# A hub stage with its startup, its loads and its row saves in another order

## The chip, the cores and the metric

The kernel runs on one core of a Trainium2 chip (trn2). The metric is device time in microseconds of one launch. The runs give a median and a range, and one more execution is taken by the hardware profiler; the profile and its trace come from that one. Engines are called as the profile calls them: PE (matrix multiply), PEld (its weight load), DVE (vector), ACT (scalar), POOL (GpSimd) and SP (which here only issues DMAs). "SPq" and "ACTq" are the DMA-issuing instructions on SP and ACT.

## The reference

The input is x (8 batches, 2048 nodes, 64 channels) and a 2048 x 2048 adjacency matrix whose entries are dense among the low-numbered nodes and sparse elsewhere. One layer of two-level graph attention is added to x, and the sum is layer-normalised:

```
mask = graph + eye(N) > 0
h = einsum('bnc,hdc->bhnd', x, Wh)              # 4 heads
out_h = softmax(where(mask, h h^T, -1e16)) h + bh
z = leaky_relu(concat of heads);  h2 = z Wo^T
out2 = softmax(where(mask, h2 h2^T, -1e16)) h2 + bo
y = layernorm(leaky_relu(out2)) * gamma + beta
result = layernorm(x + y)
```

## The kernel before

The kernel uses the sparsity. The first 56 nodes ("hub" nodes, `HUB`) attend to every node and are computed densely. The other 1992 nodes are grouped into 166 sets of 12, and for each set only up to 128 listed neighbours are fetched with an indirect DMA. There are three stages, one after the other: the hub stage (it also builds the neighbour lists), the first layer for the sets (83 pairs of sets), and the second layer. The order on each engine is the order in which the Python code issues instructions; there is no scheduler, and each engine runs its own queue in order.

**The hub stage** begins with loads. `load_x(i)` (line 449) allocates a tile of 128 nodes from a ring of ten row tiles, sets its border columns on DVE (line 451) and issues two DMAs on ACT's queue (line 453), each of 128 KB in contiguous stretches of 64 floats. `save_x(i)` (line 457) writes that tile from SP to `table1` in DRAM, from which the second stage gathers; until that write has landed, the tile's place in the ring can't be reused. Before the loop four x tiles are loaded, then `hubraw` (the adjacency rows of the hubs, line 465), the weights `wnat` and `wos` (lines 467 and 468).

`load_adj` (line 669) loads one piece of the adjacency matrix of the sets (480 KB) through SP into a ring of three `raw` buffers, which the two `hubraw` tiles share; POOL turns it into a 0/1 bf16 tile `a` (line 680) and, on each second piece, sets the diagonal (line 687). The `a` tiles come from a ring of five, which `hubm` and `hubs` share. `more(n)` issues the next n pieces. Twelve pieces make a round of 60 sets; there are 34 pieces in three rounds.

Ahead of the loop, in this order: `more(2)`; `hub_mask` (the hubs' 0/1 mask `hubm` on DVE, line 541, 16 turning matmuls into `pm`, line 545, and the two halves of `maskh`, line 548); `hub_mask_sets` (a strided copy `hubs` on ACT, line 559, 17 turning matmuls into `pms`, line 562, and `maskt`, line 566, which only the last stage reads); `weights` (lines 497 to 506: `gram`, `whT`, `woT`); `turn_x(0)` (transposes of x tile 0 into `xT`, lines 512 and 583); `hub_columns` (line 575, `yh`).

The loop has 16 iterations of two halves t. A half is `hub_scores` (matmuls `sh`, line 590; the mask subtracted on DVE, line 594, called the lift here; exp on ACT, line 597) and, one half later, `hub_values` (matmuls `oh`, line 608, into the accumulators `hubo`). Around them:

```
        if i + 4 < NB:
            load_x(i + 4)
        more(2 if i < 7 else 1)
        save_x(i)
        ...
            if t == 1 and i in (3, 6):
                make_keys(0, (i - 3) // 3, two)
                if i == 6:
                    picks = pick(0)
            if t == 1 and i in (9, 15):
                make_keys(1, (i - 9) // 6, two)
            some(3)
```

`make_keys` (line 712) packs six pieces into half of a round's keys with matmuls `pk` (line 721) and two DVE instructions (line 708). `pick(0)` (line 727) is a list of 39 DVE jobs that extract each set's neighbours: 32 with MAX8 (line 737), most of them with MATCH_REPLACE8 (line 739), one merge, one that writes `index` (line 766) and five that write `mask` (line 777). `some(3)` runs three jobs per half. After the loop the rest of the jobs run, six gathers are issued from `table1` on POOL (line 792), `own_rows` copies columns of `xT` on POOL (line 800), and `hub_end` closes the accumulators (lines 616 and 617). PSUM in this stage has two double-bank tiles with tag "s" (all short uses) and two with tag "o" (`hubo`).

Of the kernel before, what the change touches and what calls it, by code (L numbers as in the profile page):

```python
# [36 lines left out]
OP = mybir.AluOpType  # L37
# [7 lines left out]
HUB = 56  # L45
SET = 12
# [313 lines left out]
def fast_kernel(ctx: ExitStack, tc: tile.TileContext, x, adj, Wh, bh, Wo, bo, gamma, beta, out, flag):  # L360


    nc = tc.nc
    B, N, C = x.shape
    H, D, _ = Wh.shape
    P = 128
# [7 lines left out]
    NS = (N - HUB) // SET  # L374
# [20 lines left out]
    def two(name, tag="s", **kw):  # L395

        return psum.tile([P, 2, 512], F32, tag=tag, name=name, **kw)
# [27 lines left out]
    table1 = dram.tile([N, ROW], F32, name="table1")  # L425
# [11 lines left out]
    maskh = const.tile([P, NB, HUB * H], U8, name="maskh")  # L437
# [8 lines left out]

    xrow = {}

    def load_x(i):
        t = xrow[i] = rows_tile(f"x{i}")  # L450
        nc.vector.memset(t[:, :, 0:PW:PW - 1], 1.0)
        for p in range(2):
            nc.scalar.dma_start(out=t[:, :, 1 + p * D:1 + (p + 1) * D],
                                in_=x[p::2, i * P:(i + 1) * P, :].rearrange("q n c -> n q c"))

    def save_x(i):
        nc.sync.dma_start(out=table1[i * P:(i + 1) * P, :], in_=xrow[i].rearrange("n q c -> n (q c)"))
# [28 lines left out]
                                compare_op=OP.not_equal, fill=float(1 << k))  # L486
    number = early.tile([P, 2, HALFN], U16, name="number")
    nc.gpsimd.iota(number, [[1, 2], [2, SEG // 2], [SEG, HALFN // (SEG // 2)]], base=0, channel_multiplier=0)
    load_x(2)
    load_x(3)  # L490

    def weights():
        pw = two("pw")
        for h in range(H):
            for r in range(2):
                w = wnat[half(r), h, :]
                nc.tensor.matmul(pw[half(r), r, h * D:(h + 1) * D], w, w, start=True, stop=True)
                nc.tensor.matmul(pw[half(r), r, (H + h) * D:(H + h + 1) * D], w, ident[half(r), half(r)],
                                 start=True, stop=True)
        for r in range(2):  # L500
            nc.vector.tensor_copy(gram[half(r), :, half(r)], pw[half(r), r, :H * D].rearrange("c (h e) -> c h e", h=H))
            nc.scalar.copy(whT[half(r), :], pw[half(r), r, H * D:])
        po = two("po")
        for hp in range(HP):
            nc.tensor.matmul(po[:, 0, hp * D:(hp + 1) * D], wos[:, hp * P:(hp + 1) * P], ident[:D, :D], start=True, stop=True)
        nc.vector.tensor_copy(woT.rearrange("p q d -> p (q d)"), po[:, 0, :HP * D])
# [28 lines left out]
    hubm = early.tile([HUB, N], BF16, tag="a", name="hubm", bufs=5)  # L535
    HW = HUB * H
    HV = HW // 4

    def hub_mask():
        for k in range(2):  # L540
            nc.vector.tensor_scalar(hubm[:, k * NCH:(k + 1) * NCH], hubraw[k], 1.0, 0.0, OP.min, OP.max)
        nc.vector.tensor_tensor(hubm[:, :HUB], hubm[:, :HUB], identb[:HUB, :HUB], OP.max)
        pm = two("pm")
        for m in range(NB):
            nc.tensor.matmul(pm[:, m // 8, (m % 8) * HUB:(m % 8 + 1) * HUB], hubm[:, m * P:(m + 1) * P],
                             identb[:HUB, :HUB], start=True, stop=True)
        for k in range(2):
            nc.vector.tensor_scalar(
                maskh[:, k * 8:(k + 1) * 8, :].rearrange("p m (n h) -> p (m n) h", h=H),
                pm[:, k, :8 * HUB].unsqueeze(2).to_broadcast([P, 8 * HUB, H]), 0.0, 255.0, OP.is_equal, OP.mult)  # L550

    def hub_sets(b):

# [2 lines left out]
    def hub_mask_sets():  # L556
        pm = two("pms")
        cols = early.tile([HUB, NS * SET], BF16, tag="a", name="hubs", bufs=5)
        nc.scalar.copy(cols.rearrange("n (s k) -> n s k", k=SET), hubm[:, HUB:].rearrange("n (k s) -> n s k", s=NS))
        for b in range(NHB):  # L560
            s0, ns = hub_sets(b)
            nc.tensor.matmul(pm[:ns * SET, b // 9, b % 9 * HUB:(b % 9 + 1) * HUB], cols[:, s0 * SET:(s0 + ns) * SET], identb[:HUB, :HUB],
                             start=True, stop=True)
        for b0, n in ((0, 9), (9, NHB - 10), (NHB - 1, 1)):
            np_ = hub_sets(b0)[1] * SET
            nc.vector.tensor_scalar(maskt[:np_, b0:b0 + n, :].rearrange("p b n -> p (b n)"),
                                    pm[:np_, b0 // 9, b0 % 9 * HUB:(b0 % 9 + n) * HUB], 0.0, 255.0, OP.is_equal, OP.mult)
# [3 lines left out]
    def hub_columns():  # L571
        py = two("pyh")
        for t in range(2):
            for h in range(H):
                nc.tensor.matmul(py[:, t, h * 2 * HUB:(h + 1) * 2 * HUB], gram[:, h, :],
                                 xT[:, 2 * t:2 * t + 2, :HUB], start=True, stop=True)
            nc.vector.tensor_copy(yh[:, t, :].rearrange("p (n h) -> p n h", h=H),
                                  py[:, t, :H * 2 * HUB].rearrange("p (h n) -> p n h", h=H))

    def turn_x(i):  # L580
        tp = two(f"px{i}")
        turn(tp[:, 0, :], xrow[i])
        nc.scalar.copy(xT[:, :, i * P:(i + 1) * P], tp[:, 0, :].rearrange("c (q n) -> c q n", q=Q))
# [12 lines left out]
                                maskh[:, i, :].unsqueeze(1).unsqueeze(1).to_broadcast([P, 2, 2, HW]), OP.subtract)  # L596
        nc.scalar.activation(e, e, AF.Exp, bias=shifts[:, 0:1], scale=1.0)  # L597

    hubo = [two(f"oh{t}", "o") for t in range(2)]

    def hub_values(i, t):

# [109 lines left out]
    def make_keys(r, t3, new):  # L712

        n = in_round[r]
        groups = [(t, min(S10, n - S10 * t)) for t in range(3 * t3, min(3 * t3 + 3, (n + S10 - 1) // S10))]
        pk = new(f"pk{r}_{t3}")
        for h in range(2):
            c = (2 * t3 + h) * 32
            for b in range(2):
                for i, (t, ns) in enumerate(groups):  # L720
                    nc.tensor.matmul(pk[c:c + 32, b, :], powers_of(ns, t % 3), ahead[r, t][:ns * SET, h, b * 512:(b + 1) * 512],
                                     start=(i == 0), stop=(i == len(groups) - 1), tile_position=(0, c))
        for h in range(2):
            part = slice((2 * t3 + h) * 32, (2 * t3 + h + 1) * 32)
            keep_keys(keys[r % 2][part, :], pk[part], part, h)
# [64 lines left out]
    def gather(table, s, layer, new):  # L790
        t = rows[layer, s] = new(f"g{layer}_{s}")
        nc.gpsimd.indirect_dma_start(out=t.rearrange("n q c -> n (q c)"), out_offset=None, in_=table,  # L792
                                     in_offset=bass.IndirectOffsetOnAxis(ap=index[:, s:s + 1], axis=0))
# [139 lines left out]
    def more(n):  # L933

        for _ in range(n):
            if pieces:
                load_adj(*pieces.pop(0))

    more(2)
    hub_mask()  # L940
    hub_mask_sets()
    weights()
    turn_x(0)
    hub_columns()
    picks = []

    def some(n):
        for _ in range(n):
            if picks:
                picks.pop(0)()  # L950

    def turns():
        return bool(picks) and getattr(picks[0], "turns", False)

    for e in es:
        nc.vector.memset(e[:, 4 * HW:], 1.0)
    pend = None
    for i in range(NB):
        if i + 4 < NB:
            load_x(i + 4)  # L960
        more(2 if i < 7 else 1)
        save_x(i)
        if i == 2:
            nc.gpsimd.memset(rall[:, NG:, :], 1.0)
            nc.gpsimd.memset(rall2, 1.0)
            nc.gpsimd.memset(over, 0.0)
            for k in range(SET):
                nc.gpsimd.memset(bits[:, k:k + 1], N << k)
            nc.gpsimd.memset(shifts[:, 2:3], EPS)
            nc.gpsimd.memset(ones, 1.0)  # L970
            for t in rowts + xbs:
                nc.gpsimd.memset(t, 1.0)
            if last:
                make_powers6()
        for t in range(2):
            hub_scores(i, t)
            if t == 0 and i + 1 < NB:
                turn_x(i + 1)
            if pend:
                hub_values(*pend)  # L980
            pend = i, t
            if t == 1 and i in (3, 6):
                make_keys(0, (i - 3) // 3, two)
                if i == 6:
                    picks = pick(0)
            if t == 1 and i in (9, 15):
                make_keys(1, (i - 9) // 6, two)
            some(3)
    hub_values(*pend)
    while picks:  # L990
        picks.pop(0)()
    LOOK = 5
    for g in range(LOOK - 2):
        for j in range(2):
            gather(table1, 2 * g + j, 1, rows_tile)
    own_rows(0)
    own_rows(1)
    for t in range(2):
# [14 lines left out]
    picks = pick(1)  # L1013
# [3 lines left out]
    for i in range(-4, NG + 3):  # L1017
# [10 lines left out]
        if 0 <= i + 2 < NG:  # L1028
            t = held["T", 1, i + 2] = work.tile([P, 2, 512], F32, tag="xTg", name=f"xTg{i + 2}", bufs=3)
# [16 lines left out]
        if i >= 0:  # L1046
# [9 lines left out]
            if not picks and not todo3 and done < NS:  # L1056
                picks = pick(2)
# [376 lines left out]
```

## Time and profile before

| what | us |
|---|---|
| median of 3 runs (range) | 1047.05 (1044.12 to 1052.09) |
| the profiled execution, its own time | 880.76 |
| its span, first to last instruction | 878.9 |
| busy: PE, DVE, ACT, POOL | 753.0, 610.1, 514.4, 469.2 |
| hub stage in the trace | 0 to 144.4 |
| first matmul of `weights` (line 497) | 20.55 |
| first lift (line 594) | 32.78 |
| first pick (line 737) | 77.19 |
| first lift after the last pick job | 125.78 |
| last lift of the hub stage | 137.22 |

The profiled execution is 166 us shorter than the median of the runs. In the trace a line of the timeline gives start, duration, engine, source line, operation, the tile written and read, the count, and in brackets the idle time of that engine before it with what released it. A line of the busy table gives, for a stretch of time, the busy time of each engine with its count of instructions, then the clock granted to PE, the share of time in which the 16 DMA engines were busy, and the rate.

### The profile page before, as it was taken

How to read it: one execution, taken by the hardware profiler on the slowest of the kernel's cores; microseconds unless marked ns; L12 is line 12 of the kernel's file. 1: busy time of each engine (PE TensorE's matmuls, PEld its weight loads, DVE VectorE, ACT ScalarE, POOL GpSimd, SP SyncE). 2: the span in 40 equal slices, each digit the busy share in tenths (PEclk: the TensorE clock that was granted, in tenths of full speed). 3: DMA queues.
4: the chain of work that ended last, by engine and by line, in shares of the span. 5: the costliest groups of instructions: out<-in, count | busy, mean ns of one | idle time of the engine just before them, and what ended most of it. 6: DMA issues, size and time to landing. Idle time of an engine off the chain costs nothing.

```text
span 878.9 us, 42066 instructions
## 1 busy us (share of the span) xinstructions
PE 753.0 (86%) x18437; PEld 661.2 (75%) x18437; DVE 610.1 (69%) x1369; ACT 514.4 (59%) x961; POOL 469.2 (53%) x612
## 2 busy tenths in 40 slices
PE   1896777889999999999999999992999999998730
PEld 1664456778788999988999999971899999988720
DVE  3356983568888788877555555553258999998994
ACT  2342333556556667666766667651678888886821
POOL 5654141457444555655666666503777777777300
PEclk9998998999999999999999999995999999999965
DMA  8787451355434445655566665514888888888611
GB/s 167 238 218 213 129 146 48 83 142 160 109 100 118 112 125 159 162 169 153 160 168 173 160 166 162 134 28 114 246 266 253 275 275 267 266 252 242 172 46 35
DMA packets 81794, 145.22 MB, mean 165 GB/s; under 512 B 30146, under 2 KB 46466, under 8 KB 81602
## 3 DMA queue, kind: packets, MB, share of 16 engines
q0 software_dynamic: 26720, 88.55, 36.4%
q1 hardware_dynamic: 37842, 49.65, 18.7%
q10 hardware_dynamic: 17040, 4.25, 2.6%
q8 instruction: 147, 2.41, 1.1%
q14 instruction: 45, 0.37, 0.1%
HBM read 123.91 MB, written 18.48 MB: 162 GB/s over the span
## 4 chain that ended last, share of the span: by engine, by line
PE 63%; DVE 15%; DMA 7%; ACT 5%; issue 4%; SPq 3%; POOL 2%; DVEq 0%; ACTq 0%; POOLq 0%
PE t L512 11%; PE s L821 10%; PE o L846 10%; PE cat L806 6%; PE o L863 4%; PE cat L531 4%; PE cat L880 3%; PE s L1133 3%; PE o L1165 3%; PE cat L890 2%; DMA raw<-in_adj_dram 2%; SPq L1248 2%; PE sh L1277 2%; PE e L1144 2%; DMA g<-table,index 1%
## 5 line engine op out<-in xcount | busy, mean ns | idle before, releaser
L792 POOL DMA_INDIRECT g<-table,index x332 | 334.9, 1009 | 236.1 <-PE o L846 140.2
L512 PE MATMUL t<-ident,g 128*128 128x128 f32 x1328 | 182.3, 276 | 15.6 <-DMA g<-table,index 12.7
L512 PEld LDWEIGHTS t<-ident,g 128*128 128x128 f32 x1328 | 154.8, 142 | 20.0 <-issue 14.0
L826 DVE TENSOR_TENSOR e<-s,mask 128x768 f32<-128x768 f32 x83 | 79.4, 956 | 87.4 <-PE s L821 85.4
L518 ACT ACTIVATE z<-cat,bhp 128x192 f32<-128x192 f32 x166 | 60.8, 418 | 85.0 <-PE cat L531 85.0
L846 PE MATMUL o<-g,e 128*64 128x65 f32 x2656 | 97.5, 227 | 0.0
L821 PEld LDWEIGHTS s<-y,xTg 64*64 64x64 f32 x5312 | 85.2, 134 | 13.9 <-issue 13.7
L821 PE MATMUL s<-y,xTg 64*64 64x48 f32 x5312 | 95.5, 220 | 0.0
L846 PEld LDWEIGHTS o<-g,e 128*64 128x64 f32 x2656 | 85.8, 140 | 9.8
L1320 ACT COPY xTg<-t 128x1024 f32<-128x1024 f32 x83 | 80.3, 1017 | 18.1 <-PE t L512 17.3
L1030 ACT COPY xTg<-t 128x1024 f32<-128x1024 f32 x83 | 84.0, 1012 | 2.0 <-PE t L512 2.0
L833 ACT ACTIVATE e<-e,shifts 128x768 f32<-128x768 f32 x83 | 79.2, 955 | 2.1 <-DVE e L826 1.7
L812 ACT COPY y<-cat 128x384 f32<-128x384 f32 (+1 forms) x80 | 40.7, 508 | 64.0 <-PE o L863 40.1
L597 ACT ACTIVATE e<-e,shifts 128x896 f32<-128x896 f32 x32 | 33.4, 1042 | 73.0 <-DVE e L594 52.1
L680 POOL TENSOR_SCALAR a<-raw 120x1024 bf16<-120x1024 int32 (+1 forms) x34 | 38.2, 1125 | 65.1 <-DMA raw<-in_adj_dram 38.4
L806 PE MATMUL cat<-xo,gram 128*128 128x192 f32 (+1 forms) x320 | 65.6, 328 | 0.0
L853 DVE RECIPROCAL rall<-o 64x8 f32<-64x8 f32 x166 | 34.0, 205 | 42.0 <-PE o L846 40.7
L854 DVE TENSOR_TENSOR osb<-o,rall 128x512 f32<-128x512 f32 x83 | 57.4, 692 | 2.9
L1165 PE MATMUL o<-g,es 128*32 128x65 f32 x2656 | 49.1, 226 | 5.9 <-DVE y_s L1188 4.5
L806 PEld LDWEIGHTS cat<-xo,gram 128*128 128x128 f32 x320 | 53.7, 203 | 0.3 <-issue 0.2
L1165 PEld LDWEIGHTS o<-g,es 128*32 128x32 f32 x2656 | 46.1, 113 | 7.0 <-issue 4.9
L1133 PE MATMUL s<-xTg,bd 128*32 128x128 f32 x1328 | 45.4, 277 | 6.2 <-ACT bd L1124 3.5
(177 smaller groups left out, 1369.3 us busy)
## 6 DMA issues: line engine op xcount, KB each, us to landing
raw<-in_adj_dram SPq DMA_DIRECT2D x32, 480.0 KB
table<-xb SPq DMA_DIRECT2D x22, 256.0 KB
xr_s<-table SPq DMA_DIRECT2D x21, 256.0 KB
g<-table,index POOLq DMA_INDIRECT x332
table<-x SPq DMA_DIRECT2D x16, 260.0 KB
x<-in_x_dram ACTq DMA_DIRECT2D x32, 128.0 KB
table<-rowt SPq DMA_DIRECT2D x166, 24.4 KB
xb<-in_x_dram SPq DMA_DIRECT2D x164, 24.0 KB
```

Source lines behind the costliest of these rows:

```text
L512: nc.tensor.transpose(tp[:, q * P:(q + 1) * P], rows[:, q, 1:1 + P], ident)
L518: nc.scalar.activation(z[:, hp], cat[:, :, hp * n:(hp + 1) * n], AF.Identity, bias=bhp[:, hp:hp + 1], scale=1.0)
L792: nc.gpsimd.indirect_dma_start(out=t.rearrange("n q c -> n (q c)"), out_offset=None, in_=table, in_offset=bass.IndirectOffsetOnAxis(ap=ind ...
L806: nc.tensor.matmul(cat[:, k, 2 * GM:2 * GM + n], gram[:, g % 2 * 2 + k, :], held["x", g // 2][:, :n], start=True, stop=True)
L821: nc.tensor.matmul(sp[half(r), p, (q * 2 + j) * M:(q * 2 + j + 1) * M], xt[half(p), j, q, half(r)], y[half(p), (j * Q + q) * M:(j * Q + q ...
L826: nc.vector.tensor_tensor(e[:, :16 * M].rearrange("p (a q n) -> p a q n", a=2, q=Q), sp[:, :, :8 * M].rearrange("p a (q n) -> p a q n", q= ...
L833: nc.scalar.activation(e[:, :16 * M], e[:, :16 * M], AF.Exp, bias=shifts[:, 0:1], scale=1.0)
L846: nc.tensor.matmul(op[half(p), j, o0:o0 + K1], e[:, c0:c0 + 64], rw[j][:, q, sums(p)], start=True, stop=True)
L1030: nc.scalar.copy(t, held.pop(("tp", i + 2)))
L1133: nc.tensor.matmul(sp[q * 32:(q + 1) * 32, k, :], bd[u % 3][:, k, q, :], xt[:, s % 2, q, :], start=True, stop=True, tile_position=(0, q * 32))
L1165: nc.tensor.matmul(op[t * 32:(t + 1) * 32, f, k * W2 + p:k * W2 + p + K1], e[:, 2 * q + p, k, :], rw[:, q, sums(p)], start=(a == 0 and k = ...
L1320: nc.scalar.copy(t, tp)
```

## The change

- `load_x` takes an optional queue. Tiles 2 and 3 are issued on SP, each after one of the first two adjacency pieces; the other tiles stay on ACT.
- `hub_mask_sets` moves from before the loop to the end of iteration 1, and its strided copy goes from ACT to DVE.
- `pm` takes a PSUM tile of tag "o"; the two DVE instructions that make `maskh` are split: one goes after `weights`, one after `hub_columns`. The accumulators `hubo` are allocated after that.
- Adjacency pieces: 2 in iterations 0, 2, 4 and 7 to 12, 1 in iterations 1, 3, 5 and 6, none from 13. So 12 have been issued by iteration 6 and 24 by the end of the loop (before: 16 and 25).
- `save_x` is delayed: tiles 0 to 3 in iterations 5 to 8, then two tiles in each of iterations 9 to 14.
- `make_keys` runs in iterations 3, 8, 11 and 15, so that `pick(0)` starts in iteration 8; `some` takes four jobs per half.
- The first six gathers are issued in iteration 14.

```diff
-    def load_x(i):
+    def load_x(i, queue=None):
...
-            nc.scalar.dma_start(out=t[:, :, 1 + p * D:1 + (p + 1) * D],
+            (queue or nc.scalar).dma_start(out=t[:, :, 1 + p * D:1 + (p + 1) * D],
...
-    load_x(2)
-    load_x(3)
...
+    maskp = []
...
-        pm = two("pm")
+        pm = two("pm", "o")
+        maskp.append(pm)
...
-        for k in range(2):
-            nc.vector.tensor_scalar(
-                maskh[:, k * 8:(k + 1) * 8, :].rearrange("p m (n h) -> p (m n) h", h=H),
-                pm[:, k, :8 * HUB].unsqueeze(2).to_broadcast([P, 8 * HUB, H]), 0.0, 255.0, OP.is_equal, OP.mult)
+
+    def hub_mask_half(k):
+        nc.vector.tensor_scalar(
+            maskh[:, k * 8:(k + 1) * 8, :].rearrange("p m (n h) -> p (m n) h", h=H),
+            maskp[0][:, k, :8 * HUB].unsqueeze(2).to_broadcast([P, 8 * HUB, H]), 0.0, 255.0, OP.is_equal, OP.mult)
...
-        nc.scalar.copy(cols.rearrange("n (s k) -> n s k", k=SET), hubm[:, HUB:].rearrange("n (k s) -> n s k", s=NS))
+        nc.vector.tensor_copy(cols.rearrange("n (s k) -> n s k", k=SET), hubm[:, HUB:].rearrange("n (k s) -> n s k", s=NS))
...
-    hubo = [two(f"oh{t}", "o") for t in range(2)]
+    hubo = []
...
-    more(2)
+    more(1)
+    load_x(2, nc.sync)
+    more(1)
+    load_x(3, nc.sync)
     hub_mask()
-    hub_mask_sets()
     weights()
+    hub_mask_half(0)
     turn_x(0)
     hub_columns()
+    hub_mask_half(1)
+    hubo.extend(two(f"oh{t}", "o") for t in range(2))
     picks = []
+    save_at = {i: range(i - 5, i - 4) if i < 9 else range(2 * i - 14, 2 * i - 12) for i in range(5, 15)}
...
-        more(2 if i < 7 else 1)
-        save_x(i)
+        more(2 if i in (0, 2, 4) or 7 <= i < 13 else 1 if i < 7 else 0)
+        for k in save_at.get(i, ()):
+            save_x(k)
...
-            if t == 1 and i in (3, 6):
-                make_keys(0, (i - 3) // 3, two)
-                if i == 6:
+            if t == 1 and i in (3, 8):
+                make_keys(0, i // 8, two)
+                if i == 8:
                     picks = pick(0)
-            if t == 1 and i in (9, 15):
-                make_keys(1, (i - 9) // 6, two)
-            some(3)
+            if t == 1 and i in (11, 15):
+                make_keys(1, i // 4 - 2, two)
+            if t == 1 and i == 1:
+                hub_mask_sets()
+            some(4)
+        if i == 14:
+            while picks:
+                picks.pop(0)()
+            for g in range(LOOK - 2):
+                for j in range(2):
+                    gather(table1, 2 * g + j, 1, rows_tile)
     hub_values(*pend)
-    while picks:
-        picks.pop(0)()
-    LOOK = 5
-    for g in range(LOOK - 2):
-        for j in range(2):
-            gather(table1, 2 * g + j, 1, rows_tile)
```

More of the change, by code (lines that the diff above doesn't have):

```diff
@@ L953, in turns @@
         return bool(picks) and getattr(picks[0], "turns", False)
+    LOOK = 5
     for e in es:
```

## The prediction, made before the changed kernel ran

> **What bounds the kernel now.** I read first the busy table over the stages, because the change touches only the hub stage (0 to 144.4 us); then DVE's, ACT's and PE's timelines inside it; then the queue's own waits.
>
> ```profile
> 0.00:31.00 31.00, 10.96 (x93) 9.61 (x93) 8.75 (x17) 6.18 (x5) 16.92 (x39) 1.00 0.83 188
> 31.00:75.00 44.00, 38.15 (x701) 25.96 (x704) 18.95 (x27) 17.80 (x21) 21.85 (x61) 0.96 0.83 232
> 75.00:126.00 51.00, 36.20 (x665) 25.74 (x657) 47.35 (x125) 15.34 (x18) 15.08 (x20) 0.93 0.48 142
> 126.00:144.40 18.40, 13.84 (x292) 9.82 (x288) 10.53 (x14) 7.20 (x8) 5.10 (x7) 0.97 0.31 89
> ```
>
> Columns: stretch, length, then PE, PEld, DVE, ACT, POOL busy. The stage has four parts with different limits. To 31 us no compute engine is the limit: the startup waits for loads (DMA 0.83 busy). From 31 to 75, PE is busy 38 of 44: this part is PE's, with a few stalls. From 75 to 126, DVE is busy 47 of 51: the picks. Then PE's chain again.
>
> The startup's chain is in ACT's and PE's timelines:
>
> ```profile
> 15.14 3.57 ACT L559 COPY hubs<-hubm 56x1992 bf16<-56x1992 bf16 x1 [13.11 <-DMA x<-in_x_dram]
> ...
> 18.76 1.86 PE L562 MATMUL pms<-identb,hubs 56*120 56x56 bf16 x17 [10.99 <-ACT hubs L559]
> 20.55 0.48 PE L497 MATMUL pw<-wnat 64*64 64x64 f32 x4
> ```
>
> ACT can copy `hubs` only at 15.14, because its queue first issues eight x DMAs and is held there; PE sits 10.99 us with `weights` behind `pms`. From the first weights matmul (20.55) to the first lift (32.78) are 12.2 us of a chain of small steps.
>
> How early the weights could start is in SP's waits:
>
> ```profile
> SPq L675 <- DMA wos<-in_L_gnn_Wo_dram: 7.8, 1, 7.8
> ```
>
> SP issued the first raw piece at 3.72, was held for `wos`, and issued the second at 12.54. So `wos` landed near 12.5, and `wnat`, ahead of it in the queue, not later.
>
> The stall in the second part is on ACT:
>
> ```profile
> 63.45 1.04 ACT L597 ACTIVATE e<-e,shifts 128x896 f32<-128x896 f32 x1 [1.07 <-DVE x L451]
> 68.14 1.01 ACTq L453 DMA_DIRECT2D x<-in_x_dram  x2
> 69.19 1.04 ACT L597 ACTIVATE e<-e,shifts 128x896 f32<-128x896 f32 x1 [4.70 <-DMA table<-x]
> ```
>
> An x load at 68.14 waited for a row save (issued about 60.9 by the chain of waits, 7.49 us of DMA), and exp stood behind it for 4.70 us.
>
> [...] ACT was held by issuing until 15.10 us (its last startup x DMA alone held it 3.11 us), with compute behind it. [...] in the first 16 us ACT's queue took 36.4% of the 16 engines for 0.91 MB, SP's 36.6% for 1.47 MB. [...]
>
> **The change part by part**, against the profiled execution (span 878.9, own time 880.76).
>
> Startup. PE no longer waits for `hubs`; `weights` waits for `wnat`, `wos`. With x tile 3 and most of x 2 behind the weights on SP, less competes: 36.4% of 16 us is 5.8 us for about 7 x DMAs, 0.8 each; some 2.5 of them fewer before 12.5 us bring `wos` to about 10.5 (estimate; ends 9 and 12.5). From there the old chain of 12.2 us, plus one `maskh` half (3.96/2 = 1.98 us) which now stands on DVE between `yh` and the first lift. DVE was idle 1.04 us there, so about 1.0 is added: first lift at 10.5 + 12.2 + 1.0 = 23.7, where it was 32.78: 9.1 us earlier. The other half lies beside PE's `px` and `pyh` (DVE idle 4.00 there); without that cover it would cost 2.0.
>
> Mask sets in iteration 1. The copy now stands on DVE behind the lift, PE's `pms` behind the copy, `maskt` behind `pms`, the next lift behind `maskt`; `sh` of iteration 2 and all of PE wait too. I price the copy by the row of line 541 (1024 elements from SBUF to bf16 in 0.684 us): 1.33 us; the ACT row, 3.57, is the upper end. So from lift to lift 1.09 + 1.33 + 1.86 + 1.27 + 0.2 for hand-overs = 5.75 instead of a usual 2.38: +3.4 us (up to +5.6).
>
> Loop to the picks. Lifts in the second part stand at 32.78, 35.12, 37.28, 39.87, 41.87, 44.46, 46.93, 49.51: 2.38 us per half, with PE back to back. After a `make_keys` the step is 5.5 (49.51 to 55.03). Now 17 halves precede the picks, not 13: 15 x 2.38 + 5.5 + 5.75 = 46.9, and from the lift to the end of the second keys 5.4 (49.51 to 54.86). Picks start at 23.7 + 46.9 + 5.4 = 76.0, where they were at 77.19. The four extra halves (9.5) have eaten the early start, and only the absence of the stall (before, 10.2 from lift to end of keys, now 5.4) pays for it.
>
> Picks. From 77.19 to 125.78 are 48.6 us with 12 lifts among them; the same 39 jobs at four per half hold 9 lifts. DVE is the limit, a lift costs about 1.02 there: 48.6 - 3.1 = 45.5. They end at 121.5.
>
> Tail. Before, six lifts follow, the first at 125.78 and the last at 137.22: 2.29 per half. Now five: the first at 121.5, the last 9.2 later at 130.7, and the same 7.2 to the end of the stage: 137.9. Against 144.4 that is 6.5 us.
>
> Saves, pieces and queues, taken at nothing. Saves now follow the pieces on SP. Behind each stand later pieces, and on DVE the border memset of the tile that reuses its place, with all lifts behind that. Save 0 stands behind piece 11, whose raw buffer is freed by POOL's piece 8; POOL meanwhile is held at its fourth `a` tile until `hubm` is free (iteration 1, near 34 us), then by 5.2 us of memsets, so save 0 goes at about 44, while its memset is due in iteration 6, near 60. Cover: some 15 us; if it goes, DVE stops one save time, 7.5 us as seen, and again at later tiles. Raw pieces come at about 3 us each (15.35, 20.29, 22.93, 25.07, 27.23, 30.77); the 12th is due near 70. x 2 and 3 on SP hold up the second raw piece little, since it waited to 12.54 anyway. The gathers were ready when `index` was (121.44) and still are. One raw piece (POOL 1.1) moves into the next stage, beside PE.
>
> Sum: 9.1 earlier start - 3.4 mask sets + 4.8 stall gone - 9.5 for four halves more before the picks + 3.1 + 2.3 for the halves fewer in picks and tail = 6.4 us, the same within rounding. Profiled time about 874.4. The runs' median is 166 us above the profiled execution, and the trace doesn't show where. If spread evenly the gain is 7.6; if it is all slower PE, three more halves run at PE's pace and the gain is about 5. I take 6: 1041.
>
> **Rivals.** *It stays about as it was*: `wos` lands at 12.5 whatever competes (-2.0) and the strided copy takes 3.57 (-2.2): gain 2, 1045. For it: the DMA engines are busy to 0.83 in the startup anyhow.
>
> *More than the startup*: stalls like the 4.70 us on ACT are more frequent in the longer runs, and fewer saves early (before the picks 4 to 6, where 11 were; each 260 KB) remove them. Another one or two of such stalls, and `wos` at 9: 6 + 1.5 + 9 = 16, 1031. For it, DMA at 0.83 to 75 us. Against, PE is busy 38 of 44 in that part, which leaves some 6 us, of which 4.8 are counted already.
>
> *Slower*: the saves come too late. POOL's fourth `a` tile waits for `hubm`, SP is in order, DVE's memsets in iterations 6 to 11 each wait for a save. If the chain of pieces runs more than 15 us late, three or four memsets stop DVE for about 6 us: 20 lost less 6 gained, 1060. Against it: the estimated 15 us of cover.
>
> **How the numbers follow.** The forecast 0.52 (own range 1035 to 1047), about as it was 0.15, more than the startup 0.21, slower by saves 0.12. Within 1% (10.5 us, about what a measurement of this kernel can tell from no change) are the first two, less a small tail: 0.66; faster 0.22; slower 0.12. The range 1029 to 1053 leaves out half of the third and most of the fourth.
>
> **What would show it.** First weights matmul at 9 to 12.5 us, first lift near 24; a gap of 5 to 8 us between lifts in iteration 1; no exp stalled on a save; picks start near 76 with DVE busy to 121; stage end near 138. The forecast is wrong if a border memset of line 451 waits for a save, if raw pieces make `make_keys` wait, or if the later stages move.

## The result and the profile after

| | before | after |
|---|---|---|
| median of 20 runs each, one chip (range), us | 1046.93 (1042.05 to 1053.94) | 1047.37 (1038.42 to 1054.55) |
| ratio after to before, 95% interval | | 1.000 [0.9976, 1.0024] |
| the profiled execution, its own time | 880.76 | 1050.06 |
| its span | 878.9 | 1047.7 |

The change makes no measurable difference. The forecast of 6 us less was wrong; of its cases, "it stays about as it was" came true, but not by that rival's mechanism (late weights and a slow copy).

The two profiled executions can't be compared in absolute time. That of before (880.76) lies far below its runs, and the likely reason is that it comes from another chip: the same kernel before took 879.51 us (28 runs, 873.36 to 884.25) on the chip of e1 to e4 below, and 1042 to 1047 on the others. So the hub stage is compared between e1 (before) and e2 (after), profiled on one chip, and again between e9 and e10 on another. Moments in us from the start of the span:

| kernel | chip | first lift | first pick | last pick job starts | last lift | stage ends |
|---|---|---|---|---|---|---|
| e1 before | 880 us | 30.79 | 77.76 | 126.16 | 137.77 | 144.8 |
| e2 after | 880 us | 22.22 | 85.32 | 130.95 | 141.23 | 148.3 |
| e9 before | 1045 us | 31.43 | 79.52 | 129.24 | 147.08 | 154.2 |
| e10 after | 1045 us | 23.48 | 87.99 | 133.61 | 150.35 | 157.4 |
| after, the run of the result | 1045 us | 22.51 | 86.20 | 131.83 | 148.14 | 155.2 |

On both chips the first lift comes 8 to 9 us earlier, and the stage nevertheless ends 3.3 to 3.5 us later. That is the whole question: 11 to 12 us are lost between the first lift and the end.

The busy table of after, in the same stretches and columns as that of before:

```profile
0.00:31.00 31.00, 19.84 (x192) 14.91 (x192) 11.37 (x22) 5.85 (x8) 17.74 (x39) 1.00 0.86 183
31.00:75.00 44.00, 34.41 (x635) 25.15 (x630) 18.74 (x24) 15.37 (x19) 19.89 (x58) 0.88 0.78 212
75.00:126.00 51.00, 33.42 (x578) 23.22 (x574) 42.90 (x108) 13.42 (x18) 11.41 (x16) 0.89 0.45 142
126.00:155.30 29.30, 23.05 (x341) 16.12 (x341) 15.07 (x29) 8.19 (x9) 8.71 (x10) 0.78 0.27 74
```

To 31 us PE now does 19.84 us of work instead of 10.96: the earlier start is real. But from 31 to 75, the stretch that was PE's, PE is busy 34.4 us instead of 38.2, at a clock of 0.88 instead of 0.96: it does less, and does it more slowly. The pair on one chip agrees: to 31 us 12.95 (e1) and 19.34 (e2), then 37.6 at a clock of 0.93 and 35.0 at 0.84.

The earlier start, in PE's timeline of after:

```profile
7.84 0.47 PE L495 MATMUL pw<-wnat 64*64 64x64 f32 x2
...
9.53 0.49 PE L495 MATMUL pw<-wnat 64*64 64x64 f32 x4 [1.01 <-DMA wnat<-in_L_gnn_Wh_dram]
```

The first weights matmuls (line 495 here, 497 before) run at 7.84, where they ran at 20.55, and are held for the rest of `wnat` only to 9.53. PE no longer waits for `hubs`.

And the stall that the forecast took as gone, in ACT's timeline of after:

```profile
64.32 3.65 ACTq L453 DMA_DIRECT2D x<-in_x_dram  x2
68.02 1.04 ACT L598 ACTIVATE e<-e,shifts 128x896 f32<-128x896 f32 x1 [6.37 <-DMA raw<-in_adj_dram]
```

It has the form of the stall of before, which the prediction read as 4.70 us behind a row save: two x loads are issued on ACT, and exp stands behind them for 6.37 us. The bracket now names a raw adjacency piece. The chain of waits of after has that piece:

```profile
59.12 8.46 DMA raw<-in_adj_dram
```

An x load shares no buffer with a raw piece, so it doesn't need that piece's data. The trace of after ties them all the same: it keeps which semaphore an instruction waits for and when transfers signal it. Of the two loads of tile 10, in iteration 6, the first waits for a semaphore that the save of tile 3 signals, the second for one that the 17th adjacency piece signals, which SP issues in iteration 9. The first load was issued at 64.32, when the save of tile 3 had landed (64.30), and the second at 67.60, when the piece had (67.58). exp comes behind them in ACT's program: the lift that it reads was done at 63.59, and it started at 68.02.

**The stall of before was the same wait.** The releaser in a bracket is inferred from what ended close by, and in before it is the wrong transfer. SP's timeline of before, ahead of the stall:

```profile
60.06 0.80 SPq L675 DMA_DIRECT2D raw<-in_adj_dram  x1
60.91 0.52 SPq L457 DMA_DIRECT2D table<-x  x1
```

The piece is again the 17th (issued in iteration 7 there). ACT, ahead of the load of tile 10, waited for the semaphore that this piece signals: the last part of the piece landed at 68.06, ACT's wait ended at 68.08, and POOL's wait for the same piece at 68.09. The load was issued at 68.14, and the save of 60.91 landed only at 68.40. So the load never waited for that save. e1 has a stall of the same form, the load at 67.54 and exp at 68.54 after 5.94 us, with a save in the bracket too.

### The profile page after: what moved, and what is told of

Read it like the earlier page. It is cut to its first block, busy times and chain, and to the rows that moved or that the text cites. A ratio compares the mean times of both kernels' runs of the same rounds, so it can differ in the third digit from the quotient of the medians.

```text
span 1047.7 us, 42055 instructions
## 1 busy us (share of the span) xinstructions
PE 837.7 (80%) x18437; PEld 705.8 (67%) x18437; DVE 616.2 (59%) x1370; ACT 515.1 (49%) x960; POOL 463.6 (44%) x612
## 4 chain that ended last, share of the span: by engine, by line
PE 69%; DVE 9%; issue 9%; ACT 4%; DMA 4%; POOL 1%; another core or an unknown queue 1%; SPq 0%; DVEq 0%; POOLq 0%; ACTq 0%
PE t L510 16%; PE s L822 10%; PE o L847 8%; PE cat L807 5%; PE s L1144 5%; PE o L1176 3%; PE o L864 3%; PE cat L529 3%; PE cat L881 3%; PE sh L1288 2%; PE e L1155 2%; ACT xTg L1331 2%; PE cat L891 2%; DMA raw<-in_adj_dram 2%; PE oh L1310 1%
## 5 line engine op out<-in xcount | busy, mean ns | idle before, releaser
L793 POOL DMA_INDIRECT g<-table,index x332 | 330.4, 995 | 406.4 <-PE o L847 170.0
L510 PE MATMUL t<-ident,g 128*128 128x128 f32 x1328 | 198.1, 279 | 24.7 <-DMA gh<-table 10.4
L510 PEld LDWEIGHTS t<-ident,g 128*128 128x128 f32 x1328 | 157.3, 144 | 42.8 <-issue 35.1
L822 PE MATMUL s<-y,xTg 64*64 64x48 f32 x5312 | 114.5, 222 | 6.3 <-issue 5.6
L822 PEld LDWEIGHTS s<-y,xTg 64*64 64x64 f32 x5312 | 98.4, 134 | 26.0 <-issue 18.5
L1163 DVE TENSOR_TENSOR es<-e,linked 128x384 f32<-128x384 f32 (+1 forms) x42 | 23.1, 550 | 136.8 <-PE t L510 116.1
L1144 PE MATMUL s<-xTg,bd 128*32 128x128 f32 x1328 | 63.4, 305 | 31.0 <-issue 21.0
L598 ACT ACTIVATE e<-e,shifts 128x896 f32<-128x896 f32 x32 | 33.4, 1042 | 95.1 <-DVE e L595 63.5
L1144 PEld LDWEIGHTS s<-xTg,bd 128*32 128x32 f32 x1328 | 41.8, 120 | 48.1 <-issue 39.3
L681 POOL TENSOR_SCALAR a<-raw 120x1024 bf16<-120x1024 int32 (+1 forms) x34 | 38.2, 1126 | 70.1 <-PE pk L722 36.7
L1176 PE MATMUL o<-g,es 128*32 128x65 f32 x2656 | 54.9, 236 | 7.6 <-DVE y_s L1199 5.1
L595 DVE TENSOR_TENSOR e<-sh,maskh 128x896 f32<-128x896 f32 x32 | 34.8, 1088 | 42.7 <-PE sh L591 36.6
```

The source lines that it names most:

```text
L510: nc.tensor.transpose(tp[:, q * P:(q + 1) * P], rows[:, q, 1:1 + P], ident)
L822: nc.tensor.matmul(sp[half(r), p, (q * 2 + j) * M:(q * 2 + j + 1) * M], xt[half(p), j, q, half(r)], y[half(p), (j * Q + q) * M:(j * Q + q ...
L1144: nc.tensor.matmul(sp[q * 32:(q + 1) * 32, k, :], bd[u % 3][:, k, q, :], xt[:, s % 2, q, :], start=True, stop=True, tile_position=(0, q * 32))
L1176: nc.tensor.matmul(op[t * 32:(t + 1) * 32, f, k * W2 + p:k * W2 + p + K1], e[:, 2 * q + p, k, :], rw[:, q, sums(p)], start=(a == 0 and k = ...
```

## The experiments

All kernels compute the whole reference. Most line numbers differ by one between the two kernels; "lift" is the mask subtraction on DVE, as before. A wait in brackets is idle time of that engine just ahead of the instruction.

**e1 and e2: both kernels on one chip; e9 and e10: on another.** No edit.

> The unchanged kernel, for a second profile of it. The profiled execution of before had a span of 879 us where its runs take 1047. Theory A (that profile was an unusual execution, and its extra speed lies outside the hub stage): span about 1045, the hub stage still ends near 144 to 147 us, the first lift is near 33 and the extra 165 us lie in the last stage. Rival B (the hub stage too is slower in a usual execution, so the forecast was summed against the wrong base): the hub stage ends at 152 us or later.

> The changed kernel once more, for a second profile. If the 10 us that its hub stage lost after the first lift (stage end 155 us) come with the schedule, the end is again at 153 to 157 us. If they came by chance in that one execution (slow first matmuls, PE held for 4 us at 132 to 136 us, exp held 6.4 us at 68 us), the end is at 138 to 148 us.

> The unchanged kernel for one more profile, beside the next three. On a chip where it takes about 880 us its hub stage ended at 144.3 and 144.8 us. If this chip is one where it takes about 1045, the profile tells where the other 165 us are: theory, in the last stage (from the first matmul of scores2 to the end about 370 us, not 243) and the hub stage ends at 150 to 153 us, since with the old loop and another startup it ended at 151.4 there; rival, everything is slower alike, hub stage end near 172.

> The changed kernel timed again beside before. Theory: ratio depends a little on the chip: 1.000 where before takes 1045 us (as measured), 1.006 to 1.010 where it takes 880 (one run of 887 against 879.5). The hub stage ends 3 to 4 us later than before's. Rival: no difference on either kind of chip, ratio within 0.997 to 1.003 and a stage end within 2 us of before's.

e1 took 880.05 and e2 887.20 (one execution each). e9 took 1055.07 (one execution), e10 1047.69 (22 runs) against 1045.08 for before (43 runs), ratio 1.0025 [1.0001, 1.0048]. The table above has the stages; that of e2 fits neither of its two ranges, which were set from another chip. So the hub stage of after is 3.3 to 3.5 us longer on either chip. The runs of e10 fit that (2.6 us), and hardly exclude no difference. The execution of e9 is longer than each of the 43 runs beside it (1036.04 to 1051.07), so differences against its stage, here and below, may be some us off.

Where the time lies between two chips is seen in the last stage. The busy table of e1 and then that of e9, each from where its last stage begins:

```profile
637.00:880.00 243.00, 193.44 (x4928) 177.06 (x4926) 203.91 (x369) 166.84 (x298) 145.04 (x142) 0.92 0.72 213
```

```profile
692.00:1055.00 363.00, 252.76 (x4929) 206.69 (x4927) 204.87 (x370) 165.72 (x298) 135.59 (x139) 0.86 0.51 139
```

The same 4928 matmuls take 363 us instead of 243, with 139 GB/s instead of 213 and PE's clock at 0.86 instead of 0.92; DVE's and ACT's work is equal. Of the 175 us between these two executions 120 are here, about 9 in the hub stage, the rest in the first layer. What makes the chips differ was not settled, and it does not touch the comparison.

**The cost of the mask sets in iteration 1**, read in e2. DVE's timeline:

```profile
29.30 1.09 DVE L595 TENSOR_TENSOR e<-sh,maskh 128x896 f32<-128x896 f32 x1 [1.50 <-PE sh L591]
30.30 1.88 DVE L560 COPY hubs<-hubm 56x1992 bf16<-56x1992 bf16 x1
33.78 1.27 DVE L567 TENSOR_SCALAR maskt<-pms 120x504 uint8<-120x504 f32 x3 [1.60 <-PE pms L563]
...
35.58 1.09 DVE L595 TENSOR_TENSOR e<-sh,maskh 128x896 f32<-128x896 f32 x1 [0.51 <-PE sh L591]
40.03 1.09 DVE L595 TENSOR_TENSOR e<-sh,maskh 128x896 f32<-128x896 f32 x1 [3.36 <-PE sh L591]
```

From lift to lift are 6.28 us over the mask sets (forecast 5.75), and then 4.45 more where a half usually takes 2.38: 10.73 for two halves, 6.0 more than usual. The second excess is PE's, in its timeline of e2:

```profile
28.17 0.99 PE L591 MATMUL sh<-yh,xT 64*64 64x224 f32 x16
...
32.23 1.51 PE L563 MATMUL pms<-identb,hubs 56*120 56x56 bf16 x17 [1.63 <-DVE hubs L560]
33.67 1.77 PE L591 MATMUL sh<-yh,xT 64*64 64x224 f32 x16
...
36.41 2.00 PE L609 MATMUL oh<-x,e 128*64 128x65 f32 x32
...
40.90 0.99 PE L591 MATMUL sh<-yh,xT 64*64 64x224 f32 x16
```

The same sixteen `sh` matmuls take 0.99 us ahead of PE's wait for the copy, 1.77 after it, and 0.99 again at 40.90. The busy table of e2 has the clock (the third number from the end):

```profile
29.00:33.00 4.00, 2.08 (x47) 1.78 (x44) 2.88 (x2) 1.92 (x3) 2.29 (x2) 0.96 0.84 221
33.00:36.00 3.00, 3.00 (x27) 2.04 (x27) 1.72 (x5) 0.00 (x0) 2.93 (x24) 0.50 0.96 192
36.00:40.00 4.00, 4.00 (x57) 2.88 (x57) 0.67 (x1) 1.51 (x2) 3.25 (x16) 0.56 0.67 222
40.00:44.00 4.00, 4.00 (x96) 3.22 (x98) 2.20 (x3) 1.90 (x2) 3.93 (x6) 1.00 0.42 79
```

From 33 to 44 PE has no idle time, and still runs at about half its clock for 7 us (0.50 from 33 to 36, 0.56 from 36 to 40). The `sh` times agree with that (1.77 and 0.99). In the stretch ahead, from 29 to 33, the clock was 0.96 and PE was idle for 1.92 us, 1.63 of it in one piece. That this wait lowered the clock is inferred from the order in time; no run isolates it.

**e3 and e4: each half of the change alone.** e3 has the startup of after (masks, weights, x tiles 2 and 3 on SP, mask sets in iteration 1) and the loop of before; e4 the startup of before and the loop of after (pieces, saves, keys, picks, gathers).

```
e3, in after's loop
-        more(2 if i in (0, 2, 4) or 7 <= i < 13 else 1 if i < 7 else 0)
-        for k in save_at.get(i, ()):
-            save_x(k)
+        more(2 if i < 7 else 1)
+        save_x(i)
...
-            some(4)
+            some(3)
```

> Only the startup of the change: weights ahead of the mask sets, the mask sets at the end of iteration 1, x tiles 2 and 3 on SP; the pieces, saves, keys and picks of the loop as before. Theory (the early start is eaten by the later picks): the picks start 4 to 6 us earlier than before, the stage ends 4 to 6 us earlier than before, ratio 0.993 to 0.998. Rival (the loop is bound by the arrival of pieces and x tiles, not by its start): exp or make_keys waits grow by the same amount and the stage ends within 2 us of before, ratio 1.000.

> Only the loop of the change: pieces, late saves, keys at 3, 8, 11, 15, four jobs per half, gathers in iteration 14; the startup as before. Theory: the picks start at iteration 8, four halves later, some 5 us later than before, and the stage ends 2 to 6 us later, ratio 1.002 to 1.006. Rival (late saves remove waits on ACT and pay for it): the stage ends no later than before, ratio 1.000 or below.

e3: 877.38 us (22 runs), ratio 0.9979 [0.9959, 0.9999]; first lift 21.05, first pick 77.67, stage end 144.8. e4: 888.88 (7 runs), ratio 1.0091 [1.0059, 1.0122]; 30.91, 91.35, 154.4. So the loop loses 9.6 us of the stage by itself (2 to 6 were expected). The startup gains 6 with that loop (154.4 to 148.3) and next to nothing with the old one: in e3 the first lift is 9.7 us earlier and the first pick comes at the same moment as in e1, within 0.1. The lead is gone long before the picks: the lift at 52.82 stands at 53.14 in e1. Most of it went in the two halves with the mask sets, 13.0 us where 4.8 is usual. There, and once more ahead of the first keys, exp stood behind x loads, in ACT's timeline of e3:

```profile
30.26 1.04 ACT L598 ACTIVATE e<-e,shifts 128x896 f32<-128x896 f32 x1 [4.86 <-DMA x<-in_x_dram]
...
46.00 1.04 ACT L598 ACTIVATE e<-e,shifts 128x896 f32<-128x896 f32 x1 [2.75 <-DMA x<-in_x_dram]
```

The second of these holds ended with a load that was issued at 45.58. After that both kernels run alike, into the stall (exp at 69.04 after 6.77 us; in e1 at 68.54 after 5.94). The earlier start ran into waits that transfers ended.

**e5, e8 and e11: the loop's x loads on SP.** One edit each, in after (e5), in e7 below (e8) and in before (e11):

```
-            load_x(i + 4)
+            load_x(i + 4, nc.sync)
```

> The changed kernel with the x loads of the loop issued on SP as well, so that no exp stands behind an x DMA on ACT. Theory A (exp is held because ACT issues loads that wait for older transfers, 8.6 us in the second profile of the changed kernel): exp has no such wait, the hub stage ends at 141 to 146 us (148 with the change), ratio to before 0.996 to 1.002. Rival B (the loads themselves are late, whoever issues them): the wait moves to PE's transposes of x or to make_keys, and the stage ends at 147 us or later, ratio 1.004 to 1.010.

> As the run with the mask sets ahead of the weights and the loop of before, with the x loads of the loop issued on SP. Theory A (exp held by the issue of x loads is what binds the loop before the picks): picks start at 68 to 72 us, stage end at 135 to 139 us, ratio 0.990 to 0.995. Rival B (arrival of x tiles and pieces binds it): picks start at 75 us or later, and PE or make_keys waits for a DMA or for POOL instead.

> The kernel before with one edit: the x loads of the loop are issued on SP. Theory A (exp on ACT standing behind x loads is the stall before the picks, and it ate the early start): the gap of 13 to 15 us at the second keys shrinks to 10 to 11, picks start 4 to 7 us earlier (71 to 74 us), ratio 0.993 to 0.997. Rival B (it needs the early start too, since without it the loads are not ahead of time): picks start at 76 us or later, ratio 0.998 to 1.001.

e11 is the clean test, since it adds nothing else to before: 1038.04 us (22 runs), ratio 0.9939 [0.9915, 0.9962], first pick 70.42 (e9, on the same chip: 79.52), stage end 144.2 (154.2). The bytes and the other transfers are the same. ACT's timeline of e11, where the stall stood:

```profile
61.54 1.04 ACT L597 ACTIVATE e<-e,shifts 128x896 f32<-128x896 f32 x1 [1.07 <-DVE x L451]
63.54 1.04 ACT L597 ACTIVATE e<-e,shifts 128x896 f32<-128x896 f32 x1 [0.96 <-DVE e L594]
...
66.13 1.04 ACT L597 ACTIVATE e<-e,shifts 128x896 f32<-128x896 f32 x1 [1.08 <-DVE e L594]
```

No exp waits for a transfer any more. From 31 to 70 us the DMA engines even move more than in e9, 238 GB/s instead of 221, busy 0.87 instead of 0.76, and PE works 35.8 us instead of 32.1. So the stall came from loads that wait on a queue with compute behind them, not from a shortage of DMA bandwidth. The edit does two things at once: exp no longer stands behind the loads, and the loads go out on another queue, with other transfers ahead of them. Loads that stay on ACT without the wait for a piece were not tried. e8 against e7 repeats the gain: 0.9936 [0.9912, 0.9960] against 0.9987 [0.9960, 1.0014], on one chip, with the first pick at 68.91 as expected, but the stage end at 144.9 (135 to 139 expected). In e5 the same edit brings the first pick of after from 86.2 to 80.3 and the time to 0.9974 [0.9945, 1.0003]; its stage end, 150.6, missed the 141 to 146 expected. There the first pick waits 2.69 us for POOL, and another wait has come up, the one of the prediction's slower rival (total, times, longest):

```profile
DVE x L451 <- DMA table<-x: 2.5, 1, 2.5
```

**e6 and e7: the mask sets back before the loop.** `hub_mask_sets()` stands ahead of `weights()` again, with the copy still on DVE; in after (e6) and in e3 (e7).

```
     hub_mask()
+    hub_mask_sets()
     weights()
...
-            if t == 1 and i == 1:
-                hub_mask_sets()
```

> The changed kernel with the mask sets put back ahead of the weights, their copy still on DVE. Theory A (the mask sets in iteration 1 cost 6 us on the path, with the slower matmuls behind them; ahead of the weights they mostly lie under the wait for the weights): first lift at 23 to 25 us, lifts 2.0 to 2.7 us apart in iteration 1, stage end at 142 to 146 us. Rival B (what is won before the picks is given back at the later waits for loads): stage end at 147 to 149 us as with the change.

> The startup of the change with the mask sets ahead of the weights (copy on DVE), and the loop of before. Theory A (the early start was eaten by the mask sets in iteration 1): picks start at 70 to 73 us, stage end at 137 to 140 us, ratio 0.992 to 0.996. Rival B (before the picks the loop is bound by its loads: with only the startup changed the picks started at 77.7 us though the first lift was 10 us earlier): picks start at 76 to 78 us again, stage end at 143 to 145 us, ratio 0.998 to 1.000.

First lifts 23.63 and 23.42: with the copy on DVE, 1.1 to 1.2 us later than in after (22.51), so the mask sets cost little there and 6 us in iteration 1. But e6 is slower than after: 1055.34 (4 runs), ratio 1.0107 [1.0067, 1.0146], stage end 161.6, outside both of its expected ranges. ACT's timeline of e6:

```profile
40.75 7.16 ACTq L453 DMA_DIRECT2D x<-in_x_dram  x2
47.95 1.04 ACT L598 ACTIVATE e<-e,shifts 128x896 f32<-128x896 f32 x1 [15.08 <-DMA raw<-in_adj_dram]
```

Time saved ahead of an x load came back as a longer wait, 15.08 us, and more. In e4, which has the same loop, SP's issues of raw pieces waited 29.2 us for POOL's conversions (9 waits, the longest 12.1); whether the piece named here was late for that was not shown. e7, with the loop of before, took 1044.13 (12 runs), ratio 0.9987 [0.9960, 1.0014], its first pick at 78.47: of a first lift 8 us earlier than in e9, 1 us is left. Exp was held for 4.7, 7.7 and 5.2 us; the waits of e7 name a row save for the 4.7 and the 5.2 (9.9 together) and nothing for the 7.7.

**e12: what beats both kernels.** e8, with one more edit: POOL clears `cand` ahead of the loop. In e8 the keys were ready at 65.4, and the first pick waited 3.49 us, to 68.91, for POOL, which cleared `cand` only behind four conversions of pieces.

```
+    nc.gpsimd.memset(cand, 0.0)        ahead of the loop
...
-        if r == 0:
-            nc.gpsimd.memset(cand, 0.0)
```

> Mask sets ahead of the weights, loop of before, x loads on SP, and in addition POOL clears cand ahead of the loop and not at the start of the picks, where the first pick waited 3.5 us for it (keys end at 65.4, first pick at 68.9). Theory: the first pick follows the keys within 0.5 us, picks start at 65 to 66 us, stage end 3 us earlier than with the clearing in its old place, ratio 0.988 to 0.993. Rival: the picks then wait for the next pieces and the stage end doesn't move, ratio 0.993 to 0.995.

1028.67 us (6 runs), ratio 0.9831 [0.9792, 0.9869]; first pick 65.00, stage end 140.5. DVE's timeline of e12:

```profile
59.59 1.09 DVE L595 TENSOR_TENSOR e<-sh,maskh 128x896 f32<-128x896 f32 x1 [1.68 <-PE sh L591]
62.43 2.47 DVE L709 SCALAR_TENSOR_TENSOR keys<-pk,number 32x1024 f32<-32x1024 f32 x2 [1.75 <-PE pk L722]
65.00 0.43 DVE L736 MAX8 cand<-keys 128x8 f32<-128x256 f32 x1
```

From lift to pick are 5.4 us, the very figure that the prediction took for a loop without the stall. The startup pays once neither exp nor the first pick is held: the stage ends 13.7 us earlier than in e9, where x loads on SP alone (e11) gave 9.9. (In e11 the keys were ready at 70.31 and the first pick began at 70.42, so the clearing held nothing there.) The time fell by 16.4, more than expected; the 3 us beyond the stage are about as uncertain as six runs leave them.

**e13, e14 and e15: the parts of the changed loop.** e13 is e12 with the whole loop of after. e14 is e12 with the late saves alone, e15 is before with the late saves alone:

```
-        save_x(i)
+        for k in save_at.get(i, ()):
+            save_x(k)
```

> The changed kernel with the mask sets ahead of the weights, the x loads of the loop on SP and cand cleared ahead of the loop: beside the fastest kernel so far it differs only in the loop (pieces, saves, keys at 3, 8, 11, 15, four jobs per half). Theory (a, later picks cost what the PE-bound halves cost): picks start after the second keys at 24 + 46 = 70 to 73 us, stage end at 143 to 146 us on a slow chip (139.8 with the old loop), ratio 0.986 to 0.991. Rival (c, the loop cost only through the hold on ACT): stage end within 2 us of 139.8, ratio 0.981 to 0.986.

> The fastest kernel so far with the saves of the change (late), all else the same. Theory: the saves neither gain nor cost once x loads are on SP: picks start at 65 to 67 us, ratio 0.981 to 0.986. Rival b: the border memsets of x tiles 10 to 15, or the loads, wait for saves, the picks start 3 us later or more, ratio 0.987 or above; or the saves were in the way and it gains 2 us, ratio below 0.981.

> The kernel before with only the saves late. Theory: exp on ACT stands behind x loads that now wait for raw pieces in place of saves, so the stall stays in another form: picks start at 75 to 80 us, ratio 0.998 to 1.004. Rival: the saves were what held ACT (4.7 us), the stall goes, picks start at 70 to 73 us, ratio 0.994 to 0.997.

e13: 1036.61 (20 runs), ratio 0.9959 [0.9933, 0.9985], first pick 78.78, last pick job 124.65, stage end 149.0, worse than both of its expectations. Against e12, which ran on another chip, the picks begin 13.8 us later, take 45.9 us instead of 50.0, and the stage ends 8.5 later (the prediction's terms, 9.5 - 3.1 - 2.3, make 4.1). The rest is seen in DVE's timeline of e13:

```profile
61.78 1.09 DVE L595 TENSOR_TENSOR e<-sh,maskh 128x896 f32<-128x896 f32 x1 [1.37 <-PE sh L591]
68.73 0.07 DVE L451 MEMSET x<- 128x8 f32 x1 [5.86 <-DMA table<-x]
...
71.85 1.09 DVE L595 TENSOR_TENSOR e<-sh,maskh 128x896 f32<-128x896 f32 x1 [1.96 <-PE sh L591]
76.21 2.47 DVE L709 SCALAR_TENSOR_TENSOR keys<-pk,number 32x1024 f32<-32x1024 f32 x2 [3.27 <-PE pk L722]
```

A border memset waits 5.86 us for the late save of the tile whose place it takes. e14 has it too, 4.86 us, and took 1031.94 (8 runs), ratio 0.9916 [0.9879, 0.9954]; its stage ends at 143.4, 2.9 later than in e12. In after itself the memset never waits: the loop is so late, for the mask sets and the stalled exp, that the saves have landed. e15 took 1038.95 (20 runs), ratio 0.9981 [0.9958, 1.0003]. In it exp still waits once, 4.0 us, behind the load of tile 10, and the bracket now names a raw piece (load issued 66.00, exp at 67.49):

```profile
ACT e L597 <- DMA raw<-in_adj_dram: 4.0, 1, 4.0
```

So delaying the saves does not remove the stall: they were not its cause.

## Why the prediction was wrong, by its own steps

The sum of the prediction against e2 (the chip of the profile that it was made from):

| step | forecast | e2 | off by |
|---|---|---|---|
| first lift | 23.7 | 22.2 | -1.5 |
| mask sets, more than two usual halves | 3.4 | 6.0 | +2.6 |
| stalls between lifts, to the picks | 0 | 7.0 | +7.0 |
| other halves, 46.9 less the 3.4, and to the end of the keys | 48.9 | 50.1 | +1.2 |
| picks start | 76.0 | 85.3 | +9.3 |
| picks | 45.5 | 45.6 | +0.1 |
| to the last lift | 9.2 | 10.3 | +1.1 |
| stage end | 137.9 | 148.3 | +10.4 |

(The stall: 11.76 us from the lift at 63.57 to that at 75.33, less two halves of 2.38. Stage end: 141.23 and 7.1.)

*Startup*: right, and a little better than forecast; `wnat` landed by 9.53.

*"the absence of the stall (before, 10.2 from lift to end of keys, now 5.4)"* is the step that failed, with 7.0 of 10.4 us. The prediction read that an x load waited for a row save and exp for the load, and took the save as the cause; with the saves moved away the stall had to go. That exp stood behind the load was right; that the load stood behind the save was not. It waited for the 17th adjacency piece, in before (piece landed 68.06, load issued 68.14) as in after (67.58 and 67.60). ACT's timeline of e2 has the same stall:

```profile
66.92 1.04 ACT L598 ACTIVATE e<-e,shifts 128x896 f32<-128x896 f32 x1 [6.79 <-DMA raw<-in_adj_dram]
```

In after a late save came on top: the first load of tile 10 waited for the save of tile 3 (landed 64.30), the second for the piece. e15 moved only the saves, and exp still waited 4.0 us, for a raw piece by the bracket; e11 moved only the loads off ACT, and no exp waited for a transfer. The prediction had even noted that ACT was held by issuing until 15.10; it didn't carry that to the loop, where twelve tiles' loads stayed on ACT. In before the wait is seen on ACT itself, ahead of the load (it ended at 68.08, the load went out at 68.14), and the 0.6% of e11 is the price here of having exp behind such loads.

*Mask sets*: the mechanism was right and the size was off. The copy took 1.88 us for 1.33, inside its bounds (1.33 to 3.57), and the gap 6.28 for 5.75; the larger part, 2.1 us in the half behind it, is PE at half clock after its wait, of which the prediction had nothing.

*Four halves more before the picks, fewer in picks and tail*: the picks were right within 0.1 us. The trade itself is worse than forecast even without stalls: e13 against e12 loses 8.5 us of the stage where these terms gave 4.1, of which e14 gives 2.9 to the late saves.

*"Saves, pieces and queues, taken at nothing"*: in after the memsets don't wait, as forecast. But the cover of 15 us was an estimate on a schedule that did not come true; on e13's quicker one a memset waits 5.86 us. The slower rival's mechanism is thus in the change, hidden behind the two other losses.

*"More than the startup"* was wrong about the change and right about the kernel: there was time to be had (e12, 16 us), by the queue of the loads and by POOL's clearing of `cand`, not by fewer early saves.

*To the end of the run*: e2 is 6.6 us longer than e1 in span (884.8 and 878.2) and its hub stage 3.5; the other 3 arise in the first layer. One more raw piece there was forecast at nothing; that it is the cause is only argued, and one execution each is too little to say that the difference is there. On the chips of 1045 us, 2.6 of 3.3 us (e10) arrive in the time.

## What to carry to other kernels

When an engine's compute waits for a transfer that it doesn't read, look at which DMA stands ahead of it in that engine's program and what that DMA waits for. Check it by the semaphore: a releaser that a profile infers can be the wrong one, as the save was here (landed at 68.40, the load issued at 68.14). Move the issue to a queue with no compute behind it before moving the transfers; moving the saves left exp waiting (4.0 us in e15). And time saved ahead of a wait whose end is set elsewhere is no gain: follow it to the next wait before adding it up.

## What was not expected of the hardware

- One chip ran the same kernel in 880 us and others in 1042 to 1047, with the last stage at 243 and 363 us. The change's effect on the hub stage was alike on both (3.5 and 3.3 us), the level was not.
- PE ran at half clock for about 7 us after a wait of 1.63 us (clock 0.50 and 0.56, `sh` 1.77 us instead of 0.99), and the half behind that wait took about 2 us more than usual. That the wait lowered the clock is inferred, not tested.
- On the chips of 1045 us, about the time that six gathers are issued (in after from 127.67 to 135.03 on POOL), PE loses time to no wait that the trace names. PE's timeline of after:

```profile
134.87 0.35 PE L609 MATMUL oh<-x,e 128*64 128x65 f32 x4 [1.07 <-issue]
...
136.34 1.21 PE L609 MATMUL oh<-x,e 128*64 128x65 f32 x17 [0.52 <-issue]
```

There the six lifts or five after the picks take about 6 us more than on the other chip, in before (17.8 and 11.6) as in after (16.3 and 10.3). Whether the gathers are the cause stays open.
